# Attention from factors: the two halves of a score set on one row group, in two tiles each of F and G

## The chip, the cores and the metric

The kernel runs on one core of one Trainium2 chip. The metric is the device time of one execution in microseconds. Three runs of the kernel before took 5,615.98, 5,625.36 and 5,626.08 us; the median, 5,625.36, is the time before.

## What is computed

The reference is a network of four layers on an input of 4 images, 128 channels, 64 x 64 points, in float32. Layer 0 is a deformable convolution, layer 1 a convolution with a scan in two directions, layer 2 an attention by cosines, a feed-forward block and a mixture of experts; layer 3 has the attention that is changed here, and another mixture of experts. That attention, on 4,096 tokens an image with 128 channels, after a layer norm of the tokens, is

```python
f = jnp.einsum('bih,ha->bia', x, W1[:h])
g = jnp.einsum('bjh,ha->bja', x, W1[h:])
t = jnp.tanh(f[:, :, None, :] + g[:, None, :, :] + b1)
scores = jnp.einsum('bija,a->bij', t, w2[:, 0]) + b2[0]
flag = jnp.tril(jnp.ones((n_seq, n_seq), dtype=x.dtype), -1)[None, :, :]
e = jnp.exp(scores) * flag
denom = jnp.sum(e, axis=-1, keepdims=True) + 1e-10
w = e / denom
return jnp.einsum('bij,bjh->bih', w, x)
```

with 16 values of a. Every token looks at all earlier ones, so the tanh would be wanted at 16 x 4,096 x 4,096 / 2 places of each image.

## The kernel before

**The way of computing.** With E = exp(2(f + g + b1)), tanh is 1 - 2 / (E + 1), and E is a product of a factor of token i and a factor of token j. The 16 values of a are split into three sets, of 6, 5 and 5 (ATT_SETS, L67). For each set the sum of w2 / (E + 1) is written as one fraction: the common denominator is a sum over all subsets of the set (64, 32 and 32 terms), and each term is again a factor of i times a factor of j. So the denominators of a block of 128 x 512 scores are a matrix product of F (128 rows of terms by 512 tokens) with G, and the numerators one of F with N, where N is G with each row multiplied by the weights of that subset (cw). Rows 0 to 63 of these tiles belong to the first set, 64 to 95 to the second, 96 to 127 to the third. `attention_maps` (L1907) makes the maps from tokens to exponents, wf and wg, and cw, once.

**Products.** A product runs on 32 rows of the PE array, and four products on four different groups of rows can run at once. The second and third set take one product each. The first set has 64 rows and takes two, rows 0 to 31 and rows 32 to 63, whose results are added in one PSUM bank. [...]an order is needed. It goes through SyncE: a `nop` on SyncE, `between` (L2150), waits for the first half of both the denominators and the numerators (`leads`), and the second halves (`ends`) wait for that `nop`. The matmuls of float32 appear in the profile as two passes, so each product of the code has two rows there.

**Steps.** An image has eight row blocks ib of 512 tokens; row block ib has 4 ib + 3 steps (`blocks`, L2113), one for each 128 x 512 block of scores with the blocks on the diagonal cut and joined. That is 136 steps an image and 544 in all, and 7 more at the end. `step` (L2261) calls `products` (L2122) for a block, and carries older blocks on:

- den: the denominators of this block, four products into three of D's four banks. The second and third set always use banks 1 and 2. The first set uses bank 0 or bank 3 (`side` 0 or 1).
- num: the numerators of the block before, four products into num1 and num2 (three banks, one buffer).
- ScalarE: Ln of the three banks of D, into the tile r, and Exp of minus that, which is one over each denominator. A fourth quarter of the same tile holds the finished sum of an older block, so one Exp of 2,048 columns does both.
- VectorE multiplies r with num2, then num1. POOL adds the three quarters into another tile r. On the diagonal VectorE then multiplies the finished weights by the mask `keep`.
- `weigh` (L2212): one product of the weights with the tokens into acc, over the whole row block.
- `settle` (L2225), once for each row block: transposes into D's bank 3, a copy zs, and the division by the denominator in VectorE.

All engines work in program order in this stage, except that POOL, VectorE, ScalarE and TensorE wait for each other where tiles or banks demand it; `held_to` and its callers say by hand which Ln a product must wait for.

**Preparation.** The next row block's F, G and N are made in six parts (`prepare`, L2078), spread over the steps of the present row block: 0 statistics (every second block), 1 the normalised tokens v, 2 four transposes into bank 3 and the copy vT, 3 the product of wf with vT and F = exp, 4 the largest value of F for the later test of size, then the product of wg and G, 5 the largest value of G, then N = G * cw on POOL. A part that uses bank 3 (2, 3, 4, `ON_BANK`, L2258), as settle does, makes a step "taken":

```python
taken = held[-1] is not None or any(p in ON_BANK for p in parts)
side = int(last[0] == 0 and not taken and not last[1])
again = side == last[0]
```

A taken step and the one behind it have side 0. Where side is the same as in the step before (`again`), den writes the bank that the last Ln reads and waits for it. The order of the products depends on it: without `again` the second and third set of den come last; with it they come before the second halves.

The number of the part that has to be done by round r is `to` (L2283): 6 parts over all rounds of the row block, in the last row block over the rounds from the 11th.

Of the kernel before, what the change touches and what calls it, by code (L numbers as in the profile page):

```python
# [16 lines left out]
P = 128  # L17
# [45 lines left out]
ROW, NROWS = _places(ROWS)  # L63

# [23 lines left out]
class Kernel:  # L88
# [1818 lines left out]
    def attention_maps(self, ctx):  # L1907
# [5 lines left out]
        with tc.tile_pool(name="r3a", bufs=2, space=PSUM) as aux, tc.tile_pool(name="r3w", bufs=1) as wp:  # L1913
# [7 lines left out]
            wf = cp.tile([P, P], F32, name="wf")  # L1921
            wg = cp.tile([P, P], F32, name="wg")
            cw = cp.tile([P, 1], F32, name="cw")
# [3 lines left out]
            with tc.tile_pool(name="r3m", bufs=1) as mp:  # L1927

                pi = mp.tile([P, 6], I32, name="pi")
                bits = mp.tile([P, 6], F32, name="bits")  # L1930
                nc.gpsimd.iota(pi, pattern=[[0, 6]], base=0, channel_multiplier=1)
                for k in range(6):
                    nc.vector.tensor_scalar(pi[:, k:k + 1], pi[:, k:k + 1], k, 1,
                                            ALU.arith_shift_right, ALU.bitwise_and)
                nc.vector.tensor_copy(bits, pi)
                has = mp.tile([P, 2, 16], F32, name="has")
                nc.vector.memset(has, 0.0)
                for hs, a0, a1 in ATT_SETS:
                    nc.vector.tensor_copy(has[hs, 0, a0:a1], bits[hs, 0:a1 - a0])
                    nc.vector.tensor_scalar(has[hs, 1, a0:a1], bits[hs, 0:a1 - a0], -1.0, 1.0,  # L1940
                                            ALU.mult, ALU.add)
# [10 lines left out]
                for k in range(4):  # L1952
                    src = has[:, k, :] if k < 2 else wd[:, k - 2, :]
                    nc.tensor.transpose(ps[0:16, k * P:(k + 1) * P], src, self.ident)
                nc.vector.tensor_copy(sel.rearrange("p k c -> p (k c)"), ps[0:16, :])

# [3 lines left out]
                nc.vector.tensor_add(sel[:, 3, :], sel[:, 3, :], bl)  # L1960

                w2 = w2z[0:16, 24:25]
                ps = aux.tile([P, 512], F32, name="aux")
                nc.tensor.matmul(ps[:, 0:P], sel[:, 2, :], sel[:, 0, :], start=True, stop=True)
                nc.tensor.matmul(ps[:, P:2 * P], sel[:, 3, :], sel[:, 0, :], start=True, stop=True)
                nc.tensor.matmul(ps[:, 2 * P:2 * P + 1], sel[:, 1, :], w2, start=True, stop=True)
                nc.vector.tensor_copy(wf, ps[:, 0:P])
                nc.vector.tensor_copy(wg, ps[:, P:2 * P])
                nc.vector.tensor_scalar(cw, ps[:, 2 * P:2 * P + 1], 2.0, None, ALU.mult)
# [13 lines left out]
    def attention(self):  # L1983
# [14 lines left out]
        with ExitStack() as outer:  # L1998
# [7 lines left out]
            with ExitStack() as ctx:  # L2006
# [44 lines left out]
                top = cp.tile([P, NB * 8, 2], F32, name="top")  # L2051
# [26 lines left out]
                def prepare(n, q):  # L2078
# [18 lines left out]
                    out = {"v": v}  # L2097
                    for k, (to, m) in enumerate((("F", wf), ("G", wg))):
                        ps = aux()
                        aside(nc.tensor.matmul(ps, m, vT, start=True, stop=True))  # L2100
                        t = bp.tile([P, 512], F32, name=f"{to}_{q}")
                        uses[:] = [nc.scalar.activation(t, ps, AF.Exp, scale=2.0)]
                        wrote[0] = t
                        out[to] = t
                        yield
                        nc.vector.tensor_reduce(top[:, 8 * n + q, k:k + 1], t, AX.X, ALU.max)
                    w = bp.tile([P, 512], F32, name=f"N_{q}")
                    nc.gpsimd.tensor_scalar(w, t, cw, None, ALU.mult)
                    out["N"] = w
# [12 lines left out]
                def products(block, side, again, before, summed):  # L2122
# [6 lines left out]
                    now, new = spaces.pop(0), rp.tile([P, 4, 512], F32, name="r", bufs=7)  # L2129
                    spaces.append(new)  # L2130
                    if block is not None:
                        n, ib, parts, end = block
                        cs = slice(parts[0][2].start, 512)
                        dv = D[:, side:side + 3, :]
                        den = pieces[n, ib]["F"], [pieces[n, t // 4]["G"] for t, _, _ in parts], parts, \
                            D[:, 3 * side, :], [D[:, k, :] for k in (1, 2)]
                    if before is not None:
                        n0, ib0, parts0, end0, cs0, side0, r0 = before
                        n1 = pp.tile([P, 512], F32, name="num1")
                        n2 = pp.tile([P, 2, 512], F32, name="num2")  # L2140
                        num = pieces[n0, ib0]["F"], [pieces[n0, t // 4]["N"] for t, _, _ in parts0], parts0, \
                            n1, [n2[:, k, :] for k in (0, 1)]

                    def product(x, out, row, start=True, stop=True):
                        rows = slice(row, row + 32)
                        return [nc.tensor.matmul(out[:, c], g[rows, t % 4 * P:(t % 4 + 1) * P], x[0][rows, i],
                                                 start=start and k == 0, stop=stop, skip_group_check=True)
                                for k, (g, (t, i, c)) in enumerate(zip(x[1], x[2]))]

                    between = nc.sync.nop()  # L2150
                    leads, ends = [], []

                    def ready(x):
                        if x is not None:
                            for k in range(2):
                                for op in product(x, x[4][k], 64 + 32 * k):
                                    if x is den:
                                        other_sets(op, [x[0], *x[1]])

                    for to, second, todo in ((leads, False, ((den, 0), (num, 32))),  # L2160
                                             (ends, True, ((num, 0), (den, 32)))):
                        if second and again:
                            ready(den)
                        for x, row in todo:
                            if x is not None:
                                ops = product(x, x[3], row, start=not second, stop=second)
                                to += ops
                                for op in ops:
                                    if x is den:
                                        first_set(op, side, [x[0], *x[1]])  # L2170
                        if not second:
                            ready(num)
                        elif not again:
                            ready(den)
                    for op in leads:
                        tc.add_manual_dep(between.ins, op.ins.name, ENDED, reason="one bank, other rows")
                    for op in ends:
                        tc.add_manual_dep(op.ins, between.ins.name, ENDED, reason="one bank, other rows")
# [31 lines left out]
                acc = [None]  # L2210

# [44 lines left out]
                spaces = [rp.tile([P, 4, 512], F32, name="r", bufs=7) for k in range(2)]  # L2256
                held = [None] * len(later)
                PARTS, ON_BANK = 6, (2, 3, 4)  # L2258
# [230 lines left out]
```

## Time and profile before

| What | Value |
|---|---|
| Median of three runs | 5,625.36 us |
| The profiled execution, its own time | 5,626.52 us |
| Its span | 5,624.8 us |
| Mean granted clock of TensorE in the span | 0.944 |
| TensorE busy | 5,034.6 us (90%) |
| VectorE busy | 3,967.9 us (71%) |
| ScalarE busy | 3,095.8 us (55%) |
| POOL busy | 3,025.3 us (54%) |
| Attention of layer 3, 3,072 to 5,238 us: TensorE busy | 2,031.49 us of 2,166 |
| the same, ScalarE | 1,806.89 us |
| the same, POOL | 1,398.51 us |
| the same, VectorE | 1,286.40 us |
| the same, granted clock | 0.97 |

The profile is of one execution. Busy time is the time in which at least one instruction runs on the engine, so four products at once count once. PE are the matmuls, PEld the loads of their stationary operand. A row of the timeline gives start, length, engine, line, operation, the tile written and the tiles read, the shape, the count of instructions that were put together, and in brackets how long the engine had stood idle and which engine and tile released it. L81 is the line of the helper that records every operation of this stage, so groups are told apart by their tiles: D<-F,G are the denominators, num<-F,N the numerators, r<-D the Ln, r<-r the Exp on ScalarE and the sums on POOL, r<-r,num the products on VectorE. "SPq" is SyncE's queue.

### The profile page before, as it was taken

Reading aid. Unit: us, or ns where it says so; the run is one execution under the profiler, and the core shown is the slowest. Engines: PE = TensorE matmul, PEld = TensorE weight load, DVE = VectorE, ACT = ScalarE, POOL = GpSimd, SP = SyncE. Lnnn points to the kernel's source line nnn. Section 1 sums busy time; section 2 is a strip of 40 time slices with the busy share of each in tenths; the row PEclk is TensorE's granted clock in tenths of the full one; section 3 lists DMA queues with packets and bytes.
Section 4 is the critical chain, followed back from the end, with each engine's and each line's share of the span. In section 5 each row is a group of like instructions: output and inputs, shape, how many; then the busy total and the mean of one; then the engine's idle time right before and its main releaser. Section 6 shows DMA issues by size and latency. Waiting matters only on the chain. (4 is left out here: it accounts for less than half of the span.)

```text
span 5624.8 us, 62917 instructions
## 1 busy us (share of the span) xinstructions
PE 5034.6 (90%) x21582; PEld 2263.2 (40%) x21582; DVE 3967.9 (71%) x7776; ACT 3095.8 (55%) x3721; POOL 3025.3 (54%) x2995
## 2 busy tenths in 40 slices
PE   6898988879999859999787999899989998999787
PEld 3454444436656523333443333333333333333343
DVE  6888988758876577886697655566566565665796
ACT  1122222146655445555421788878878887889431
POOL 0525344314444334544498666666666665667597
PEclk8999999989989779999898999999999999999899
DMA  5545454300000110000000000000000000000001
GB/s 173 129 128 127 130 129 121 94 6 3 14 16 16 43 40 1 1 1 1 6 31 30 1 1 1 1 1 1 1 1 1 1 1 1 1 1 1 5 1 60
DMA packets 66746, 185.23 MB, mean 33 GB/s; under 512 B 13158, under 2 KB 16038, under 8 KB 64744
## 3 DMA queue, kind: packets, MB, share of 16 engines
q1 hardware_dynamic: 55792, 163.68, 9.9%
q0 software_dynamic: 6272, 12.86, 1.4%
q10 hardware_dynamic: 4344, 4.50, 0.3%
q8 instruction: 174, 2.85, 0.2%
q14 instruction: 164, 1.34, 0.1%
HBM read 131.63 MB, written 49.36 MB: 32 GB/s over the span
## 5 line engine op out<-in xcount | busy, mean ns | idle before, releaser
L81 POOL TENSOR_TENSOR r<-r 128x512 f32<-128x512 f32 (+1 forms) x1088 | 1349.2, 1240 | 750.8 <-DVE r L81 688.3
L81 DVE TENSOR_TENSOR r<-r,num 128x1024 f32<-128x1024 f32 (+1 forms) x1088 | 964.6, 926 | 626.7 <-PE num L81 555.6
L81 PE MATMUL num<-F,N 32*128 32x512 f32 (+3 forms) x4608 | 1227.1, 614 | 70.2 <-DVE r L81 27.9
L81 PE MATMUL D<-F,G 32*128 32x512 f32 (+3 forms) x4608 | 1247.3, 607 | 33.6 <-ACT r L81 29.9
L81 ACT ACTIVATE r<-r 128x2048 f32<-128x2048 f32 (+4 forms) x610 | 1018.4, 1679 | 50.9 <-POOL r L81 3.8
L81 ACT ACTIVATE r<-D 128x1536 f32<-128x1536 f32 (+1 forms) x544 | 767.3, 1410 | 263.8 <-PE D L81 213.6
L81 PE MATMUL acc<-pr,ident 128*128 128x512 f32 x1600 | 748.3, 618 | 76.2 <-DVE pr L81 76.2
L81 PEld LDWEIGHTS D<-F,G 32*128 32x128 f32 x4608 | 415.6, 187 | 487.8 <-issue 344.9
L81 PE MATMUL acc<-r,v 128*128 128x512 f32 (+3 forms) x1152 | 608.0, 615 | 2.4 <-DVE aT L81 2.4
L1885 PE MATMUL pex<-w_expert_w,vT 128*128 128x512 f32 x1024 | 489.6, 617 | 79.5 <-DVE x L1888 79.4
L81 PEld LDWEIGHTS num<-F,N 32*128 32x128 f32 x4608 | 357.1, 186 | 468.5 <-SPq L81 340.1
L1895 POOL TENSOR_TENSOR x<-x 128x512 f32<-128x512 f32 (+2 forms) x576 | 472.5, 820 | 105.8 <-DVE x L1888 75.8
L81 PEld LDWEIGHTS acc<-pr,ident 128*128 128x128 f32 x1600 | 309.1, 198 | 435.9 <-issue 339.8
L81 DVE TENSOR_TENSOR pr<-v,wt 128x2560 f32<-128x2560 f32 x160 | 452.5, 2833 | 30.1 <-PE acc L81 24.3
L81 PE MATMUL pff<-hid,w_ffn_w2T 128*128 128x512 f32 x1024 | 468.2, 600 | 0.0
L81 POOL DMA_INDIRECT px<-tab,idx x196 | 331.8, 1693 | 227.8 <-DVE idx L81 159.2
L1888 DVE TENSOR_TENSOR x<-pex,gate 128x1024 f32<-128x1024 f32 x256 | 308.8, 1212 | 61.8 <-POOL X L1896 49.9
L81 POOL TENSOR_TENSOR X<-X,sl 128x512 f32<-128x512 f32 x32 | 87.7, 2740 | 491.8 <-ACT sl L81 491.8
L81 PEld LDWEIGHTS acc<-r,v 128*128 128x128 f32 x1152 | 177.1, 191 | 392.5 <-POOL r L81 217.3
L81 ACT ACTIVATE hid<-phh,cols 128x512 f32<-128x512 f32 x320 | 198.9, 685 | 223.9 <-PE phh L81 223.9
L1885 PEld LDWEIGHTS pex<-w_expert_w,vT 128*128 128x128 f32 x1024 | 183.2, 193 | 330.3 <-DVE x L1888 181.6
L81 POOL TENSOR_TENSOR Y<-y,tm 128x64 f32<-128x64 f32 x256 | 115.9, 473 | 323.4 <-DVE w L81 160.7
(562 smaller groups left out, 7139.3 us busy)
## 6 DMA issues: line engine op xcount, KB each, us to landing
v<-tab SPq DMA_DIRECT2D x320, 256.0 KB
oms<-omw SPq DMA_DIRECT2D x32, 432.0 KB
omr<-oms SPq DMA_DIRECT2D x32, 432.0 KB
X<-in_x_dram SPq DMA_DIRECT2D x8, 1024.0 KB
tab<-vb SPq DMA_DIRECT2D x64, 128.0 KB
o<-o SPq DMA_DIRECT2D x32, 256.0 KB
oin<-o SPq DMA_DIRECT2D x32, 256.0 KB
kept<-X SPq DMA_DIRECT2D x4, 2048.0 KB
```

Source lines behind the costliest of these rows:

```text
L81: return lambda *args, **kwargs: self.tc.keep_in_program_order(op(*args, **kwargs))
L1885: nc.tensor.matmul(pex[:, 4 * h:4 * h + 4, :], vT[:, k, :], ew[:, 512 * h:512 * (h + 1)], start=True, stop=True)
L1888: nc.vector.tensor_tensor(x, pex, gate[:, k, :].unsqueeze(2).to_broadcast([P, NE, P]), ALU.mult)
L1895: nc.gpsimd.tensor_tensor(x[:, 0:w, :], x[:, 0:w, :], x[:, w:2 * w, :], ALU.add)
```

## The change

The first set is split by its sixth member instead of by rows. Tile F0 and G0 hold, on rows 0 to 31, the 32 subsets without that member, F1 and G1 those with it. Rows 32 to 63 hold the same once more, multiplied by cw in G: so rows 0 to 31 serve the denominators and rows 32 to 63 the numerators of the first set. Rows 64 to 127 hold the second and third set in both; G0 keeps them as they are, for the denominators, and G1 has them multiplied by cw, for the numerators. N is gone: POOL multiplies G0 and G1 in place by two columns cw, which are 1 where nothing is to be multiplied.

The two halves of the first set are then two products on the same 32 rows, added in one bank one behind the other. The `nop` on SyncE and the waits for it are gone. In a step without `again` the order of the products is den half 0, num half 0, num's other sets, den half 1, num half 1, den's other sets. With `again` it is num half 0, num's other sets, den half 0, den half 1, num half 1, den's other sets.

A piece needs four products of a map with vT, four Exp, four reductions for the test of size and two products on POOL, where it needed two, two, two and one. There are eight parts instead of six: 2 transposes and vT, 3 F0, 4 F1, 5 G0, 6 G1 and the product of G0 with cw, 7 the product of G1. Parts 2 to 6 use bank 3. F0 and F1 have three buffers in turn, G0 and G1 one for each of the eight row blocks. The steps are the same, 544 and 7.

```diff
-                    for k, (to, m) in enumerate((("F", wf), ("G", wg))):
+                    for k, (to, m) in enumerate((("F", wf[0]), ("F", wf[1]), ("G", wg[0]), ("G", wg[1]))):
                         ps = aux()
                         aside(nc.tensor.matmul(ps, m, vT, start=True, stop=True))
-                        t = bp.tile([P, 512], F32, name=f"{to}_{q}")
+                        t = bp.tile([P, 512], F32, name=f"{to}{k % 2}" + (f"_{q}" if to == "G" else ""),
+                                    bufs=1 if to == "G" else 3)
                         uses[:] = [nc.scalar.activation(t, ps, AF.Exp, scale=2.0)]
...
                         nc.vector.tensor_reduce(top[:, 8 * n + q, k:k + 1], t, AX.X, ALU.max)
-                    w = bp.tile([P, 512], F32, name=f"N_{q}")
-                    nc.gpsimd.tensor_scalar(w, t, cw, None, ALU.mult)
-                    out["N"] = w
+                        if to == "G":
+                            nc.gpsimd.tensor_scalar(t, t, cw[k % 2], None, ALU.mult)
...
-                    between = nc.sync.nop()
...
-                    for op in leads:
-                        tc.add_manual_dep(between.ins, op.ins.name, ENDED, reason="one bank, other rows")
-                    for op in ends:
-                        tc.add_manual_dep(op.ins, between.ins.name, ENDED, reason="one bank, other rows")
+                    def first(x, half):
+                        if x is not None:
+                            product(x, x[3], 0 if x is den else 32, half, start=half == 0, stop=half == 1)
+
+                    def others(x):
+                        if x is not None:
+                            for k in range(2):
+                                product(x, x[4][k], 64 + 32 * k, 0 if x is den else 1)
+
+                    if again:
+                        first(num, 0)
+                        others(num)
+                        first(den, 0)
+                    else:
+                        first(den, 0)
+                        first(num, 0)
+                        others(num)
+                    first(den, 1)
+                    first(num, 1)
+                    others(den)
...
-                PARTS, ON_BANK = 6, (2, 3, 4)
+                PARTS, ON_BANK = 8, (2, 3, 4, 5, 6)
```

In `attention_maps` the maps are made twice, for the two values of the sixth member:

```diff
+                for b in range(2):
+                    nc.vector.memset(bits[:, 5:6], float(b))
+                    for hs, a0, a1 in ATT_SETS:
+                        nc.vector.tensor_copy(has[hs, b, 0, a0:a1], bits[hs, 0:a1 - a0])
...
+                for b in range(2):
+                    ps = aux.tile([P, 512], F32, name="aux")
+                    for k, m in enumerate((wf, wg)):
+                        nc.tensor.matmul(ps[:, k * P:(k + 1) * P], maps[:, k, :], sel[:, 2 * b, :],
+                                         start=True, stop=True)
+                        nc.vector.tensor_copy(m[b], ps[:, k * P:(k + 1) * P])
+                    nc.tensor.matmul(ps[:, 2 * P:2 * P + 1], sel[:, 2 * b + 1, :], w2, start=True, stop=True)
+                    nc.vector.memset(cw[b], 1.0)
+                    for hs in ((slice(32, 64),), (slice(32, 64), slice(64, 128)))[b]:
+                        nc.vector.tensor_scalar(cw[b][hs, :], ps[hs, 2 * P:2 * P + 1], 2.0, None, ALU.mult)
```

The largest values are kept in four columns of `top` instead of two. Everything outside the attention of layer 3 and its maps is as it was, one line further down.

## The prediction

> **What bounds the kernel now.** I read the slices of the page first (TensorE granted nearly full speed from 3,150 us on, no DMA to speak of), then the attention stage by itself, since nearly all of the change is there: its first product starts at 3,079.9 us and its last sum at 5,236 us, about 2,166 us of the span. The costliest groups of ScalarE in that stretch, by shape (line, operation, count | busy us, mean ns | idle before):
>
> ```profile
> L81 ACT ACTIVATE r<-r 128x2048 f32<-128x2048 f32 x478 | 913.3, 1911 | 44.9 <-ACT r L81 1.5
> L81 ACT ACTIVATE r<-D 128x1536 f32<-128x1536 f32 x512 | 741.8, 1449 | 248.2 <-PE D L81 213.6 <-DVE vT L81 19.9 <-DVE r L81 8.3
> ...
> L81 ACT ACTIVATE F<-D 128x512 f32<-128x512 f32 x32 | 18.7, 583 | 24.0 <-PE D L81 24.0
> ```
>
> Each step has one Ln (r<-D) and one Exp (r<-r). The Ln waits for TensorE in 214 us of the stage: one engine is full in some steps, the other in others. So I took the timeline of one ordinary step, late in an image (start, length, engine, operation, count):
>
> ```profile
> 5151.12 1.45 ACT L81 ACTIVATE r<-D 128x1536 f32<-128x1536 f32 x1 [1.48 <-PE D L81]
> ...
> 5152.01 0.69 PE L81 MATMUL D<-F,G 32*128 32x512 f32 x1
> ...
> 5152.66 1.91 ACT L81 ACTIVATE r<-r 128x2048 f32<-128x2048 f32 x1
> 5153.27 0.18 PEld L81 LDWEIGHTS num<-F,N 32*128 32x128 f32 x1 [0.94 <-SPq L81]
> ...
> 5154.34 1.13 PE L81 MATMUL acc<-r,v 128*128 128x512 f32 x2
> 5154.50 1.45 ACT L81 ACTIVATE r<-D 128x1536 f32<-128x1536 f32 x1
> ...
> 5155.39 0.69 PE L81 MATMUL D<-F,G 32*128 32x512 f32 x1
> ```
>
> A step is three rounds of TensorE: four row groups at once (from 5152.01), after SyncE's signal the second four (5153.27), then acc (5154.34), and the next step at 5155.39. The intervals are 1.26, 1.07 and 1.05 us: SyncE's hop costs 1.26 - 1.07 = **0.185 us** a step, and the step is 3.38. ScalarE in the same stretch: Ln to Exp 1.542, and from Exp to the next Ln at least 1.815 wherever nothing else holds it, together **3.357 us**. The ordinary step is thus bound by TensorE with ScalarE 0.025 us behind it. That is the main fact of this case: the hop can give back 0.185, but an ordinary step only shows 0.025 of it.
>
> The other kind is a step that must write D where the Ln before still reads ("again", L2266), with an auxiliary product behind it:
>
> ```profile
> 4115.78 1.45 ACT L81 ACTIVATE r<-D 128x1536 f32<-128x1536 f32 x1
> ...
> 4117.28 0.69 PE L81 MATMUL D<-F,G 32*128 32x512 f32 x1 [0.54 <-ACT r L81]
> ...
> 4118.53 0.18 PEld L81 LDWEIGHTS num<-F,N 32*128 32x128 f32 x1
> ...
> 4119.74 1.45 ACT L81 ACTIVATE r<-D 128x1536 f32<-128x1536 f32 x1 [0.51 <-PE D L81]
> ...
> 4120.56 1.02 PE L81 MATMUL D<-vT,wf 128*128 128x512 f32 x2
> ...
> 4121.51 0.69 PE L81 MATMUL D<-F,G 32*128 32x512 f32 x1
> ...
> 4123.10 0.58 ACT L81 ACTIVATE F<-D 128x512 f32<-128x512 f32 x1
> 4123.96 1.45 ACT L81 ACTIVATE r<-D 128x1536 f32<-128x1536 f32 x1 [0.29 <-PE D L81]
> ```
>
> From Ln to Ln 3.96 us: TensorE starts when the Ln ends and needs both rounds; then, with the product of F between, 4.21. Third, after each new row block three steps with masked columns (4.59, 4.24, 5.06) and one after settle (4.92) wait for VectorE, which frees num late; TensorE's two rounds and the Ln follow. Reading all 544 Ln starts and sorting the steps by the rules of step: row blocks 3 to 7 hold 296 ordinary steps (mean 3.42), 34 again behind a product (4.22), 30 other again (4.02), 100 steps of masks and settle; blocks 0 to 2 take 409 us for 84 steps.
>
> **The change part by part.** *The hop.* Both halves of den's first set now run on rows 0 to 31, of num's on 32 to 63, so their order comes from TensorE itself. A trace has no such pair; bounds: 0.185 us a step is gained, or nothing, if the second half's weights wait for the first half. The Trainium skill ("TensorE: Matmul & The Clock Gate", part 3, "The mechanism") speaks for nothing: weight loads overlap running matmuls only when their row groups differ. A load is 0.18 us (5153.27 above), so by the rule the hop is replaced by its like (a second weight buffer, which the same section also names, would lift it). But in the again step den's other sets go on rows 64 to 127 right behind num's, their weights load at 4117.83 us while those rows are busy, and they start at 4118.26, 0.43 us behind num's last pass. I take the row: 0.185. SyncE's queue holds only these signals in the stage, so nothing behind them moves. By the rule the sum below would be 36 us worse. Where it is on the path in blocks 3 to 7: 64 again steps and 100 of masks and settle, 164 x 0.185 = **-30**. Ordinary steps: 244 x 0.025 = **-6**.
>
> *Two products more per piece.* 32 pieces now make F0, F1, G0, G1: 64 more products (0.95 us of TensorE: 4120.56 to 4121.51), 64 more Exp of 0.58, 64 more reductions of 0.68 on VectorE, 32 more POOL products of 1.57. POOL has 0.74 us free in a step of 3.38 and N's step took 3.38 to 3.40 before, so POOL's is nothing (now it also waits for the reduction of the same tile, which ends before POOL's own two sums of that step do); uncovered it would be 50 us. All 64 Exp on the path would be 37 us, all products 61.
>
> *The bank.* Parts 2 to 6 of 8 use D's fourth bank instead of 2 to 4 of 6, and a step with such a part, and the one behind it, must take side 0. Walking the loop by its own rule for `to`, again steps go from 147 to **241**: per image, by row block, 2, 5, 7, 4, 3, 6, 6, 5 before and 2, 7, 8, 10, 10, 8, 8, 9 after. Of the 94 new ones, 28 fall on steps of masks or settle and cost nothing there: the wait for VectorE ends later than the Ln (second Ln at 4049.12, num's products at 4049.82). 14 are in blocks 0 to 2, below. 52 replace ordinary ones at 3.39. 18 of these have no product ahead: Ln 1.45, two rounds of 1.07 and two signals, 3.78, +0.39 each: **+7**. 34 stand behind a product: TensorE needs acc 0.97, product 0.95, two rounds 2.14, 4.03 with no lead; ScalarE 1.542 + 1.816 + 0.598 = 3.96. An ordinary step now leaves TensorE 0.15 us ahead, so I take 4.00, between the two: 34 x 0.61 = **+21**, and **-1** on the 34 of that kind there were. Putting num ahead of den in again steps moves num's products before the Ln's end, but Ln needs den's two rounds after it: nothing.
>
> *Row blocks 0 to 2*, followed step by step. Block 0 gets three parts a step: F0, F1, G0 behind each other in one bank, each waiting for the Exp of the one before (1.0 + 0.6 us and signals), but transposes and vT leave a step earlier: +1 an image. Block 1: vT no longer stands behind the mask: -2. Block 2: G0 now meets settle in one step and waits for zs, as the transposes do in block 4 before (5.31 against 3.94): +1.4, less the hop: +1.2 net. Together **+1**. The meeting of block 4 moves to block 6, nothing.
>
> *The rest.* Reductions and vT that fall into masked steps lengthen VectorE's chain there by 0.68 in some six places: **+4** (nothing to 20, if each of 28 were on the path). The maps take some 14 more operations of 0.16 us once: **+2**.
>
> Sum: -30 - 6 + 7 + 21 - 1 + 1 + 4 + 2 = **-2**. The profiled execution took 5,626.5 us (span 5,624.8), 1.2 above the median, so 5,624.5 there and **5,623** as a median: no change. What a measurement can tell from no change is about 0.2%, 11 us.
>
> **Rivals.** *Faster: the stalls at the start of the images go.* Blocks 0 to 2 take 409 us for 84 steps, 317 if each were a clean again step of 3.78. TensorE stands for 3 us there (4160.6 to 4163.6, for vT) and is then granted half speed; such spells sum to some 75 us from 3,150 us on, most of them at these places. If vT's earlier start ends the stalls, a third of the 92 us goes: about 5,592. Against it: three products in a row bring gaps of 1 us each. *Slower: the bank decides.* If added again steps cost the 0.6 us of 3.96 to 4.03 everywhere, masked steps too, 94 x 0.6 = 56 instead of 28: 5,651. It decides from 36 / 94 = 0.38 us per added again step. For it: again behind again leaves TensorE no lead. *The order costs as much as the hop*: the weights wait, -36 becomes 0: 5,659.
>
> **How the numbers follow.** The sum's case 0.43, spread of 12 us either way (0.10 of it faster, 0.27 same, 0.06 slower); stalls go 0.33; the bank 0.16; the weights 0.08. Faster 0.43, same 0.27, slower 0.30. The range reaches to the middle of both sides: 5,588 to 5,655; the sum's own is 5,611 to 5,635.
>
> **What would show it.** Ln to Ln 3.36 in ordinary steps with no idle before the Ln; second round 1.07 behind the first; again steps 3.78, behind products 3.96 to 4.03; 241 of them; block 0 longer, block 1 shorter. Second rounds 1.25 behind the first would make the weights' case; ordinary steps at 3.38 too. A granted clock near 1.00 through the first blocks would make the faster one.

## The result, and the profile after

The median went from 5,628.13 us (10 runs, 5,611.88 to 5,641.41) to **5,599.39 us** (10 runs, 5,581.55 to 5,613.62): a ratio of 0.9947, 95% interval 0.993 to 0.9965, so 29 us faster. The profiled execution has a span of 5,599.5 us, 25.3 below the one of before. The page of the changed kernel begins so:

```profile
span 5599.5 us, 62830 instructions
...
PE 4991.9 (89%) x21718; PEld 2404.9 (43%) x21718; DVE 4016.3 (72%) x7854; ACT 3113.9 (56%) x3785; POOL 3073.1 (55%) x3027
```

TensorE is busy 43 us less although it has 136 more passes (21,718 against 21,582), 128 of them for the doubled preparation; every other engine is busier, by 18 to 48 us. The groups of ScalarE in the attention of layer 3, by shape (line, operation, count | busy us, mean ns | idle before, and what ended it):

```profile
L82 ACT ACTIVATE r<-D 128x1536 f32<-128x1536 f32 x512 | 738.8, 1443 | 199.4 <-PE D L82 174.2 <-DVE vT L82 14.0
...
L82 ACT ACTIVATE G<-D 128x512 f32<-128x512 f32 x64 | 37.2, 581 | 10.2 <-PE D L82 10.1
L82 ACT ACTIVATE F<-D 128x512 f32<-128x512 f32 x64 | 37.2, 581 | 21.7 <-PE D L82 21.7
```

The idle time before the Ln fell from 248.2 to 199.4 us, and ScalarE took on 37 us of Exp for the preparation. Now the timeline of an ordinary step:

```profile
5144.13 1.43 ACT L82 ACTIVATE r<-D 128x1536 f32<-128x1536 f32 x1
5144.39 0.69 PE L82 MATMUL D<-F,G 32*128 32x512 f32 x1
...
5144.93 0.59 PE L82 MATMUL D<-F,G 32*128 32x512 f32 x1
...
5145.35 0.59 PE L82 MATMUL D<-F,G 32*128 32x512 f32 x1
...
5146.68 1.12 PE L82 MATMUL acc<-r,v 128*128 128x512 f32 x2
...
5147.48 1.43 ACT L82 ACTIVATE r<-D 128x1536 f32<-128x1536 f32 x1
5147.73 0.69 PE L82 MATMUL D<-F,G 32*128 32x512 f32 x1
```

The two rows at 5144.39 and 5144.93 are the two passes of the first half, the one at 5145.35 begins the second half on the same rows. It stands 0.96 us behind the first half, where it stood 1.26 behind in the kernel before; and acc comes 1.33 us after that row. Both rounds together take 5146.68 - 5144.39 = 2.29 us here, since den's other sets wait until the Ln at 5144.13 has left their banks (1.43 us later). TensorE has time for that now: the Ln has no idle time before it. Where TensorE is late the rounds are shorter, as the step that writes the bank of the Ln before ("again"), behind an auxiliary product, and the ordinary step after it show:

```profile
3908.59 1.43 ACT L82 ACTIVATE r<-D 128x1536 f32<-128x1536 f32 x1
...
3908.76 1.02 PE L82 MATMUL D<-vT,wg 128*128 128x512 f32 x2
...
3910.08 0.69 PE L82 MATMUL D<-F,G 32*128 32x512 f32 x1
...
3910.61 0.59 PE L82 MATMUL D<-F,G 32*128 32x512 f32 x1
3910.61 0.18 PEld L82 LDWEIGHTS D<-F,G 32*128 32x128 f32 x1 [0.17 <-issue]
...
3912.41 1.44 ACT L82 ACTIVATE r<-D 128x1536 f32<-128x1536 f32 x1
...
3913.04 0.69 PE L82 MATMUL D<-F,G 32*128 32x512 f32 x1
...
3914.01 0.59 PE L82 MATMUL D<-F,G 32*128 32x512 f32 x1
...
3914.97 1.13 PE L82 MATMUL acc<-r,v 128*128 128x512 f32 x2
```

From Ln to Ln it is 3.82 us, 4.21 before. The ordinary step behind it has both rounds in 3914.97 - 3913.04 = **1.93 us**, against 1.26 + 1.07 = 2.33 before. The second half begins at 3914.01, so the two rounds take 0.97 and 0.96 us, where each took 1.07 before and the signal came on top: the passes on rows 0 to 31 follow each other by 0.53, then 0.43 and 0.43, where every round before began anew with 0.53. The 0.40 us are more than twice what the hop was priced at.

All 544 Ln starts, sorted as in the prediction, give this for row blocks 3 to 7 (medians, us from Ln to Ln):

| Step | before | after | predicted |
|---|---|---|---|
| ordinary | 3.38 | 3.34 | 3.36 |
| again, no product ahead | 3.96 | 3.59 | 3.78 |
| again, behind a product | 4.21 | 3.84 | 4.00 |
| first step of a row block, blocks 5 to 7 | 3.32 | 2.22 | not named |
| the step behind settle | 4.92 | 4.92 | 4.74 (4.92 less the hop) |

The fourth row was not foreseen. The step before a new row block is only half as wide (768 columns of Ln). (In the code num is two blocks behind den, not one: `waiting` has two places.) Here is the first step of row block 6 in the second image, in the kernel before, from the half Ln to the next full one:

```profile
3937.20 0.81 ACT L81 ACTIVATE r<-D 128x768 f32<-128x768 f32 x1
...
3938.08 0.69 PE L81 MATMUL D<-F,G 32*128 32x512 f32 x1
...
3939.34 0.71 PE L81 MATMUL D<-F,G 32*128 32x512 f32 x3
...
3940.56 1.45 ACT L81 ACTIVATE r<-D 128x1536 f32<-128x1536 f32 x1 [1.15 <-PE D L81]
```

and the same place after:

```profile
3936.19 0.69 PE L82 MATMUL D<-F,G 32*128 32x512 f32 x1
3936.29 0.79 ACT L82 ACTIVATE r<-D 128x768 f32<-128x768 f32 x1
...
3938.51 1.45 ACT L82 ACTIVATE r<-D 128x1536 f32<-128x1536 f32 x1
```

ScalarE needs only 2.22 us for the half step. Before, TensorE's full step of 3.38 stood in its place (1.15 us idle before the Ln); after, TensorE has started the next block 0.1 us before the half Ln, out of a lead it has gained in the steps before, and the Ln waits for nothing. All first steps of blocks 3 to 7 together went from 66.3 to 49.5 us.

### The profile page after: what moved, and what is told of

Same layout as the page of the kernel before. It is cut to its first block, busy times and chain, and to the rows that moved or that the text cites. A ratio compares the mean times of both kernels' runs of the same rounds, so it can differ in the third digit from the quotient of the medians.

```text
span 5599.5 us, 62830 instructions
## 1 busy us (share of the span) xinstructions
PE 4991.9 (89%) x21718; PEld 2404.9 (43%) x21718; DVE 4016.3 (72%) x7854; ACT 3113.9 (56%) x3785; POOL 3073.1 (55%) x3027
## 5 line engine op out<-in xcount | busy, mean ns | idle before, releaser
L82 PE MATMUL D<-F,G 32*128 32x512 f32 (+3 forms) x4608 | 1218.8, 589 | 1.9 <-POOL G L82 1.0
L82 PE MATMUL num<-F,G 32*128 32x512 f32 (+3 forms) x4608 | 1084.5, 604 | 105.4 <-DVE r L82 101.6
L82 PEld LDWEIGHTS D<-F,G 32*128 32x128 f32 x4608 | 507.2, 189 | 327.4 <-issue 217.2
L82 PEld LDWEIGHTS num<-F,G 32*128 32x128 f32 x4608 | 394.4, 187 | 410.9 <-DVE r L82 239.5
```

The lines of the kernel that those rows point to most:

```text
L82: return lambda *args, **kwargs: self.tc.keep_in_program_order(op(*args, **kwargs))
```

## Where the time went

The attention, from first Ln to last, went from 2,141.5 to 2,106.8 us, -34.7. By place: row blocks 0 to 2 -2.1; then, in row blocks 3 to 7, first steps -16.8, second and third +4.1, the fourth to ninth (masks and settle) -5.5; and from the tenth on, 70 steps that are again now and were not +22.6, 30 that were and are -11.6, 26 that were and are ordinary now -19.3, the other 154 ordinary ones -6.1. The stretch ahead of the first Ln was 13.3 us longer in this execution and the one behind the last 3.9 shorter, which makes the 25.3 of the spans. Of the 13.3, some 6 belong to the change: from the first product of a map with vT to the first Ln it is 15.6 us, 9.9 before, for the first piece needs four products and four Exp before the first step can begin, instead of two. (With these 6 the change is -29, as in the medians.) The rest has no cause that the record shows: that first product came at 3,065.9 to 3,092.0 us over all kernels here, in no order of the edits. So stages, not spans, are compared below, beside medians.

## The experiments

Two theories were open. One: the hop is worth what was measured at it, and the doubled preparation takes most of it back. The other: the gain is somewhere else, in the new order of the products or in the stalls at the start of the images.

### The hop put back, and the preparation halved

`e_hop` is the changed kernel with a SyncE signal again between the first and second halves:

```diff
+                            if row < 64 and half == 0:
+                                tc.add_manual_dep(between.ins, op.ins.name, ENDED, reason="hop")
+                            elif row < 64:
+                                tc.add_manual_dep(op.ins, between.ins.name, ENDED, reason="hop")
...
+                    between = nc.sync.nop()
```

> The changed kernel with SyncE's hop put back between the first and the second halves of the first set; nothing else differs, and the result does not need it. Theory Q (queue: what the change gains is that the second round of products stands in TensorE's queue right behind the first and its passes follow at 0.43 us instead of 0.53, so the hop cost more than its own 0.185): again steps go from 3.59 back to 3.96, those behind a product from 3.84 to 4.21, ordinary ones from 3.34 to 3.38, the first step of a row block from 2.2 to 3.3; about 116 x 0.37 + 244 x 0.04 + 20 x 1.1 = 75 us more, 5,675. Theory H (hop alone: 0.185 a step, the rest of the gain comes from the new order of the products in again steps): again 3.78 and 4.03, about 30 us more, 5,630.

Measured: 5,711.17 us (4 runs), ratio 1.0159 (1.0129 to 1.0189); the stage 2,209.5, which is 102.7 over the changed kernel (112 in the medians). Theory Q had the kind right and the size too small, by 36 us. The timeline of one step of it:

```profile
5144.15 0.69 PE L82 MATMUL D<-F,G 32*128 32x512 f32 x1
...
5145.41 0.18 PEld L82 LDWEIGHTS D<-F,G 32*128 32x128 f32 x1 [0.94 <-SPq L82]
...
5146.48 1.13 PE L82 MATMUL acc<-r,v 128*128 128x512 f32 x2
```

1.26 and 1.07 us, exactly the kernel before. With the signal the first pass of the second round takes 0.53 again until the next; without it that round follows the passes ahead of it at 0.43. Again steps are back at 3.95 and 4.27, ordinary ones at 3.38, the first steps at 67.1 us instead of 49.5.

`e_halfprep` asks the other side: the changed kernel with F1 and G1 not made. F0 and G0 stand in for them, so part of the denominators and numerators is left out, but every product of a step runs as in the changed kernel.

```diff
-                    for k, (to, m) in enumerate((("F", wf[0]), ("F", wf[1]), ("G", wg[0]), ("G", wg[1]))):
+                    for k, (to, m) in enumerate((("F", wf[0]), ("G", wg[0]))):
...
-                        out[to].append(t)
+                        out[to] += [t, t]
...
-                PARTS, ON_BANK = 8, (2, 3, 4, 5, 6)
+                PARTS, ON_BANK = 6, (2, 3, 4)
```

> F1 and G1 are left out: each piece makes one F and one G (six parts, bank 3 in parts 2 to 4 as before), and F0 and G0 stand in for F1 and G1 in all products; the number of products, Ln and Exp in the steps stays. It prices the doubled preparation. If added again steps and added products cost what the trace of the changed kernel shows for ordinary row blocks (0.25 for an again step, 0.50 with a product ahead, over 3.34): 18 x 0.25 + 34 x 0.50 = 22 us less there, some 10 more in masked steps and blocks 0 to 2: 5,568. If they are covered: 5,595 to 5,600. If the half-speed spells of the masked steps are due to the doubled parts as well: 5,555.

Measured: 5,555.69 us (4 runs), ratio 0.9883 (0.9862 to 0.9905); the stage 2,062.0. So the hop and the closer rounds are worth 79.5 us of the stage (72 of the medians) with the preparation of before: row blocks 0 to 2 -26, first steps -20, and from the tenth step of a row block on, again steps -21.5 and ordinary ones -11.6. The doubled preparation costs 44.8 (43.7 of the medians), of which row blocks 0 to 2 have 24 and the steps from the tenth on 19. The change is **-80 + 45** in the stage, not the -36 + 34 of the prediction.

The two prices depend on each other. `e_hop`, with the hop and the doubled preparation, stands 68 us above the kernel before; so beside the hop the doubled preparation costs 68 and not 45, and beside the doubled preparation the hop is worth 103 and not 80. More again steps make the signal dearer: 41 of the 103 us lie in the 100 again steps from the tenth on.

The 5,555 that one branch of the expectation named was hit for another reason than it gave. In the fourth to sixth steps of row blocks 4 to 7 TensorE stood at half clock for 20.5 us here and for 23.9 in the changed kernel, against 4.9 in the kernel before and 3.4 in `e_hop`: in these executions the spells came with the closer rounds and not with the doubled preparation.

### The order of the products

`e_denfirst` is the changed kernel with den's first half always ahead; `e_b_numfirst` the kernel before with num ahead in again steps, and its signal kept.

```diff
-                    if again:
-                        first(num, 0)
-                        others(num)
-                        first(den, 0)
-                    else:
-                        first(den, 0)
-                        first(num, 0)
-                        others(num)
+                    first(den, 0)
+                    first(num, 0)
+                    others(num)
```

> The changed kernel with one order of the products in all steps: den's half 0 first, also in again steps, where it waits for the Ln at the head of TensorE's queue with num behind it. Theory Q: the two rounds still follow each other closely, so again steps stay at 3.59 to 3.62 and the time at 5,600 within 5 us. Theory H: the new order is what shortened the again steps, they go to 3.78 (3.84 stays where a product lies ahead), 116 steps x 0.1 to 0.19, 5,612 to 5,620.

> The kernel before with only the order of the again steps changed: num's lead and its other sets before den's lead, as in the changed kernel; SyncE's hop stays. Theory Q: den's two rounds still come after the Ln with the hop between, again steps stay at 3.96 and 4.21, time as before, 5,628 within 6 us. Theory H: again steps fall to 3.78, 64 x 0.18 = 12 us less at least, 5,615.

Measured: 5,599.14 us (7 runs), ratio 0.9949 (0.9932 to 0.9965), beside 0.9947 for the changed kernel; and 5,630.51 us (12 runs), ratio 1.0004 (0.9992 to 1.0016). Again steps are at 3.59 and 3.84 in the first, 3.92 and 4.24 in the second. The order is worth nothing in either layout, and is no part of the gain.

### The parts in the masked steps

In the changed kernel the fourth to sixth step of a row block, those that the masks make long, have become dearer in row blocks 4 to 7: 221.1 us against 215.3, although the hop is gone. In block 6, three of them took 4.28, 4.24 and 5.06 to 6.77; in block 7, where no part falls there, 4.28, 4.24 and 4.04. Two kernels move the parts behind these steps. `e_late` spreads those of blocks 4 to 6 from the tenth step on (block 7 has its own behind them already), `e_pack` puts those of blocks 4 to 7 into eight steps in a row from the tenth (from the twelfth in block 7). The code and the expectations of these two count rounds from nought: their 9th and 11th are the tenth and twelfth step.

```diff
-                    first = 4 + LAG if ib == 7 else 0
+                    first = 4 + LAG if ib == 7 else 9 if ib > 3 else 0
```

```diff
                         to = -(-PARTS * max(r - first + 1, 0) // (rounds - first))
+                        if ib > 3:
+                            to = min(PARTS, max(r - max(first, 9) + 1, 0))
```

> The changed kernel with the parts of row blocks 4 to 6 spread as before but from the 9th round on, clear of masks and settle; 249 again steps. Masked steps: first to eighth round of these blocks from 32 to 34.5 us to block 7's 31.4. Against it, again steps and the four copies v stand in the open. If masked steps are lengthened by the parts in them: 5,590. If the parts were free there: 5,605.

> The changed kernel with the eight parts of row blocks 4 to 7 in eight steps behind each other, from the 9th round (in block 7 from the 11th), clear of the steps of masks and settle; 219 again steps instead of 241. If the bank's price is the number of again steps (0.25 each, 0.50 with a product ahead), 22 fewer save 6 to 10 us and the masked steps become those of block 7, another 5 to 8: 5,585. If parts behind each other wait for each other as in block 0 (bank, Exp, next product), each product costs 1 us more, 16 blocks x 4 x 0.5: 5,630.

Measured: `e_late` 5,606.41 us (16 runs), ratio 0.9965 (0.9949 to 0.998); `e_pack` 5,575.82 us (4 runs), ratio 0.9906 (0.9877 to 0.9935). The median of `e_late` alone would say that the masked steps are indifferent to the parts. The Ln starts of blocks 4 to 7 say otherwise:

| us in row blocks 4 to 7 | changed kernel | `e_late` | `e_pack` |
|---|---|---|---|
| steps 4 to 6 (masks) | 221.1 | 202.5 | 201.0 |
| steps from the tenth on | 895.6 | 915.4 | 904.3 |
| again steps in the whole stage | 241 | 249 | 219 |

Both take about 20 us out of the masked steps. `e_late` pays them back behind, where its parts stand apart and each makes two again steps; packed, a part's second again step is the next part's first. The 20 us are the price of all eight parts there. What the doubling added is less: `e_halfprep`, with six parts in their old places, stands at 217.3 in these steps, 3.8 below the changed kernel.

### The mask on POOL

The masks keep VectorE waiting for ScalarE 171.2 us in the changed kernel, and TensorE behind it. `e_mask_pool` and `e_b_mask_pool` are the changed kernel and the one before with the mask multiplied by POOL, which has just made the tile it multiplies:

```diff
-                                nc.vector.tensor_mul(ready_e[4][:, ds], ready_e[4][:, ds], keep)
+                                nc.gpsimd.tensor_tensor(ready_e[4][:, ds], ready_e[4][:, ds], keep, ALU.mult)
```

> The changed kernel with the diagonal's mask multiplied on POOL instead of VectorE; nothing else. If the steps of masks are long because VectorE stands at the mask until the Exp ends, with the products of num behind it (4.28, 4.24, 4.04 in rounds 3 to 5), they fall towards 3.4 to 3.6: 28 blocks x 2 to 2.5 us, 5,540. If the sums on POOL become what acc waits for, they stay near 4: 5,590.

> The kernel before with the mask on POOL, the same edit. If masked steps are bound by VectorE there too, they fall from 4.59, 4.24, 5.06 towards 3.5: 5,565. It tells whether the change is worth more or less without the masked steps: with theory Q, which sets it at about 80 us less 45 of preparation, the difference to the changed kernel with the same edit stays at 25 to 45 us.

Measured: 5,512.58 us (4 runs), ratio 0.9785 (0.9749 to 0.982), and 5,520.0 us (4 runs), ratio 0.9805 (0.9772 to 0.9837). The groups of the numerators and of the mask, first in the changed kernel:

```profile
L82 PE MATMUL num<-F,G 32*128 32x512 f32 x3840 | 980.8, 643 | 92.4 <-DVE r L82 88.7
...
L82 DVE TENSOR_TENSOR r<-r,keep 128x128 f32<-128x128 f32 x128 | 64.6, 524 | 171.2 <-ACT r L82 171.2
```

then in `e_mask_pool`:

```profile
L82 PE MATMUL num<-F,G 32*128 32x512 f32 x3840 | 967.9, 636 | 47.0 <-DVE r L82 44.4
...
L82 POOL TENSOR_TENSOR r<-r,keep 128x128 f32<-128x128 f32 x128 | 57.2, 458 | 67.7 <-ACT r L82 65.3 <-DVE r L82 2.1
```

POOL's wait is the smaller, and it holds up almost nobody (what waits for the mask itself there waits 4.5 us in all). VectorE, freed of it, multiplies by num earlier, and TensorE waits half as long for num's banks, 44.4 us instead of 88.7. The mask's mean of 524 ns on VectorE hides a spread, too: the median is 293, but the one at 4,052.22 us, between two masked steps, took 1.12 us; on POOL all take 447 to 494 ns. What makes some slow on VectorE was not asked. In row blocks 6 and 7 the three long steps fall from 4.28, 4.24 and 4.04 or more to 3.34, 3.16 and 3.34 us. This one line is worth 87 us to the changed kernel and 108 to the one before, three times the change itself and more than either expectation had (5,540 and 5,565). But with it the change is worth only 7 us in the medians, and the intervals overlap (the stages of the two profiled executions differ by 19). The expectation had it stay at 25 to 45, which makes a new question: why does the same change bring 29 us beside one mask and next to nothing beside the other?

### Is the cover gone?

In row blocks 0 to 2 the change brought -2.1 us with the mask on VectorE and **+27.9** with the mask on POOL; everywhere else it brought -33 and -47. One theory: in those short row blocks the doubled preparation lay beside the waits for the masks, and is bare once they are gone. `e_half_mask_pool` is `e_halfprep` with the mask on POOL (the same part of the computation is left out).

> The changed kernel with the diagonal mask on POOL, and with the preparation at its old size: F1 and G1 are not made, F0 and G0 stand in for them in both halves of the first set, so part of the denominators is left out. The pair with the masks on POOL (before 5,520, changed 5,512.6) showed a gain of only 7 us where the pair with the masks on VectorE showed 29. Theory A, the cover is gone: the doubled preparation of row blocks 0 to 2 lay beside the waits for VectorE's mask and is now bare, while the hop is worth what it was, some 80 us: about 5,440, so that the doubled preparation costs some 72 us here against 45 with the masks on VectorE. Theory B, the hop is worth less once the masked steps are short, and preparation costs its 45: about 5,468.

Measured: 5,416.96 us (4 runs), ratio 0.9634 (0.9609 to 0.9658); the stage 1,934.5. That is the first theory, and beyond it: the hop is worth 103 us of the medians (101.1 of the stage, 24.4 of them in row blocks 0 to 2), and the doubled preparation costs 96 (82.2 of the stage, 52.3 of them in row blocks 0 to 2, where it cost 23.9 with the mask on VectorE). The timeline of `e_mask_pool` shows it bare, in the third step of the second image, between the Ln at 3,615.36 and the half Ln at 3,624.30 us, with F0, F1 and G0 to make:

```profile
3618.72 0.58 ACT L82 ACTIVATE F<-D 128x512 f32<-128x512 f32 x1
...
3619.35 1.13 PE L82 MATMUL D<-vT,wf 128*128 128x512 f32 x2 [2.13 <-ACT F L82]
3620.52 0.60 ACT L82 ACTIVATE F<-D 128x512 f32<-128x512 f32 x1 [1.22 <-PE D L82]
...
3621.17 1.12 PE L82 MATMUL D<-vT,wg 128*128 128x512 f32 x2 [0.69 <-ACT F L82]
3622.24 0.69 PE L82 MATMUL D<-F,G 32*128 32x256 f32 x2
3622.33 0.60 ACT L82 ACTIVATE G<-D 128x512 f32<-128x512 f32 x1 [1.22 <-PE D L82]
...
3624.30 0.81 ACT L82 ACTIVATE r<-D 128x768 f32<-128x768 f32 x1 [1.37 <-PE num L82]
```

Product, Exp, product, Exp, product through one bank: TensorE and ScalarE wait for each other in turn, and the step's own products come at 3622.24. Ln to Ln it takes 8.9 us; the kernel before with the same mask needs 5.8 there. In row block 1 the statistics and v of a piece now fall into one step, and TensorE waits for v:

```profile
3634.37 0.30 ACT L82 ACTIVATE rstd<-rstd,eps 128x8 f32<-128x8 f32 x1 [2.91 <-DVE rstd L82]
...
3635.35 1.24 PE L82 MATMUL D<-ident,v 128*128 128x128 f32 x4 [2.61 <-DVE v L82]
...
3637.06 1.22 PE L82 MATMUL D<-F,G 32*128 32x512 f32 x1
...
3638.91 1.07 PE L82 MATMUL D<-F,G 32*128 32x512 f32 x3
```

After the 2.61 us of standing still the row of three products takes 1.07 us, where the like takes 0.70 in the kernel before with the same mask: TensorE is granted half its clock from 3,635.8 to 3,642.7 us. These two steps together are 12.75 us from Ln to Ln; in the kernel before with the same mask 8.36.

So not all of the 52 us is the preparation's own work. In row blocks 0 to 2 TensorE stood at half clock for 53.8 us in `e_mask_pool`, for 28.6 in the kernel before with the same mask and for 22.9 in `e_half_mask_pool`; with the mask on VectorE the halved and the doubled preparation had it alike, 77.7 and 77.6. Passes on the same rows follow by 0.85 us at half clock and by 0.43 at full, so as an estimate at most half of the 31 us that `e_mask_pool` has above `e_half_mask_pool`, some 15, is lost to the clock. That is up to half of the 28 us by which the doubled preparation became dearer in these row blocks. No run here tells the two apart.

### What beats both

`e_best` is the changed kernel with the mask on POOL and packed parts, `e_b_pack_mask` the kernel before with the same two edits (six parts).

> The changed kernel with the diagonal mask on POOL and with the eight parts of row blocks 4 to 7 packed into eight steps one behind the other, from the tenth step of the row block. If the two savings add, 5,512.6 less the 24 us of packing: about 5,489. If part of what packing saved was that it kept parts out of the masked steps, which are short now, about 5,500.

> The kernel before with the same two edits: the mask on POOL, and its six parts of row blocks 4 to 7 packed from the tenth step. Again steps only go from 147 to 141 by the loop's own rule, so if packing saves through their number, about 5,515, and the changed kernel keeps the rest as its own gain. If packing saves by keeping parts together whatever the number, about 5,500.

Measured: 5,507.47 us (4 runs), ratio 0.9794 (0.9761 to 0.9827), and 5,508.65 us (4 runs), ratio 0.9801 (0.9771 to 0.9831). The savings do not add: with the masked steps short, taking the parts out of them saves 9.3 us instead of 20 and the steps behind pay 8.5. And the change is worth 1 us beside these two edits, which the runs cannot tell from nothing (12.6 in the stages of the two profiled executions, less the 6 ahead of them). The changed kernel came out above both times that were expected, the kernel before between its two. The last kernel, `e_early`, moves the bare preparation. In images 1 to 3 a piece is made one row block sooner: row block 7 of the image before makes two pieces, and row blocks 0 and 1 share one.

```diff
+                ahead = (x for piece in order[1:] for x in prepare(*piece))
...
+                        if ib == 7:
+                            to = base + min(2 * PARTS, max(r - 3 - LAG, 0)) if n + 1 < NB else done
+                        elif ib > 3:
+                            to = base + min(PARTS, max(r - 8, 0))
+                        elif n and ib == 0:
+                            to = base + PARTS + r + 1
+                        elif n and ib == 1:
+                            to = base + 3 - (-(PARTS - 3) * (r + 1) // rounds)
+                        else:
+                            to = base - (-PARTS * (r + 1) // rounds)
...
```

> The changed kernel with the mask on POOL and packed parts, as in the run at 5,507, and in images 1 to 3 the preparation moved one row block ahead: row block 7 of the image before makes two pieces (16 parts in a row from its twelfth step), row blocks 0 and 1 share one. If the bare preparation of row blocks 0 to 2 is what eats the change's gain, row blocks 0 and 1 of images 1 to 3 come down from some 53 us an image to some 40, and eight more parts in row block 7 cost 2 to 3 us an image: about -31, 5,476. If those row blocks are held by something else (the pipeline's own start at an image, the transposes of settle), they stay and the run is at 5,507 or above it.

Measured: **5,470.17 us** (5 runs), ratio 0.9719 (0.9701 to 0.9737), 37 us below `e_best`, 129 below the changed kernel. Row blocks 0 and 1 of images 1 to 3 came down from 159.7 to 111.4 us, and row block 7 of the images ahead of them went up from 324.6 to 333.9. Here, too, the clock has a share: TensorE stood at half clock for 40.1 us in row blocks 0 to 2, for 70.4 in `e_best`. The step of row block 1 that took 6.6 us takes 3.9 here, with one product beside its own:

```profile
3611.97 1.45 ACT L82 ACTIVATE r<-D 128x1536 f32<-128x1536 f32 x1 [0.77 <-PE D L82]
...
3612.79 1.02 PE L82 MATMUL D<-vT,wf 128*128 128x512 f32 x2
...
3615.86 1.45 ACT L82 ACTIVATE r<-D 128x1536 f32<-128x1536 f32 x1
```

Whether the kernel before would gain as much from the same move was not tried; its preparation is the smaller, and its row blocks 0 and 1 stood at 130.9 us in images 1 to 3 with the mask on POOL.

## Why the prediction was right, and where its steps were not

The forecast was 5,623 in a range of 5,588 to 5,655; the time is 5,599, in the range, but faster by 0.5% where the sum said no change. The sum was -36 + 34; the runs show -80 + 45 in the stage and +6 ahead of it. Both sides were too small, and 44 us of error on the one met 17 on the other. The sum's own spread, 5,611 to 5,635, missed; the wide range held since it reached halfway to the rivals, so luck has a part in it.

**The hop, -30 - 6.** The mechanism was right: no signal, no wait for weights (the rival that rested on one rule of the Trainium skill falls: the second half's pass follows at 0.43 us on the very rows that are in use). The step that failed in it is the term "**0.185**". It took off the signal and left both rounds at 1.07 us, where they measure 0.97 and 0.96. The 0.43 stood in the prediction's own row (den's other sets, 0.43 behind num's last pass), used to show that weights do not wait, and not used to price the rounds. 0.185 for the signal and about 0.1 for each of the two rounds make the 0.4 that was measured. The places were too few as well: first steps of row blocks (-20 us in `e_halfprep`) and row blocks 0 to 2 (-26) were given nothing or little, while 100 steps of masks and settle were given 18 of the 30 us and gave 3.5 (fourth to ninth steps, `e_halfprep`). In row block 7 the three masked steps went from 4.59, 4.24 and 4.04 to 4.28, 4.24 and 4.04: only one of the three became shorter, for the chain through VectorE's mask holds the others.

**Again steps, +7 + 21 - 1.** Their durations were 0.16 to 0.19 us too long in the forecast, mostly for the same reason (and the forecast's 4.03 for TensorE is 4.06 when its terms are added), and so was their price over an ordinary step: 3.59 - 3.34 = 0.25 and 3.84 - 3.34 = 0.50, not 0.39 and 0.61. At these prices the 18 and 34 net added ones make 22 us, not 28.

**Row blocks 0 to 2, +1.** Measured -2.1, but this is a gain of 26 and a cost of 24 (`e_halfprep`). Block 1 shrank as foreseen (156.6 to 148.1 us, -8.5 where -2 an image makes -8). Block 0 grew by more than foreseen (63.8 to 73.5, 9.7 for 4), and block 2 shrank (187.7 to 184.4) where 5 more were expected.

**Parts in masked steps, +4.** This held: 3.8 us in row blocks 4 to 7 (221.1 against 217.3 in `e_halfprep`), from one execution of each. That all parts together cost 20 there, old and new, was no part of the sum.

**The first piece, put at nothing.** Its two more products and two more Exp lie bare ahead of the first step, 5.7 us; the sum had only +2 for the maps.

**POOL, nothing.** Held in the ordinary step: 3.34 us is ScalarE's time, with no idle time before its Ln, while POOL has 100.0 us of products with cw instead of 50.1.

**The rivals.** "Stalls go" named a time close to the measured one, 5,592, but not the cause: the three short row blocks gave 2 of its 31 us, and time at half clock from 3,150 us to the end of the attention rose from 75 to 92 us. "The bank decides" needed the hop's whole 36 us to be eaten by 94 again steps; the hop was worth 80. "The order costs as much as the hop" is refuted by the 0.43 us.

What stays open: the split of the stage's -35 among single steps is from one execution of each kernel, and the masked steps with parts differ among images (5.06 or 6.77 in the same step), by spells at half clock whose start is not explained step by step. How much of the preparation's price with the mask on POOL is such spells is open as well.

## What to carry to other kernels

A signal through another queue between two rounds of matmuls costs more than its own latency: here it also kept the rounds 0.1 us longer each, since every round's first pass took 0.53 us and not 0.43; price the whole of both rounds from a row where such products already follow each other without a wait. Work that costs nothing beside a wait is bare when that wait is removed, so the worth of two edits is measured together: here the change was worth 29 us beside one mask and 7, within the noise, beside the better one. And where a stage has short and long row blocks, work that is due "by the next block" may be cheaper in the long ones ahead: here that brought 37 us.

## What the hardware showed

Products on different groups of rows need not start in program order. In the again step of the changed kernel den's second half is ahead of num's second half in the program:

```profile
3910.61 0.59 PE L82 MATMUL D<-F,G 32*128 32x512 f32 x1
...
3910.67 0.59 PE L82 MATMUL num<-F,G 32*128 32x512 f32 x1
...
3910.68 0.95 PE L82 MATMUL D<-F,G 32*128 32x512 f32 x3
...
3911.10 0.59 PE L82 MATMUL num<-F,G 32*128 32x512 f32 x1
```

Rows 0 to 31 are busy with den's first half until its second pass, at 3910.61; num's second half on rows 32 to 63 starts at 3910.67, 0.37 us ahead of den's, at 3911.04 (the last of the three that the row of 3910.68 puts together; the other two are den's other sets). The Trainium skill ("TensorE: Matmul & The Clock Gate", part 3, "The mechanism") has matmuls start and end in the program's order; here the starts keep it within a group of rows only, and the measurement decides. (The ends of matmuls are modelled in the profile, so they say nothing.)

And weights for rows in use are loaded ahead of time. Passes of 512 columns on the same rows follow by 0.43 us, and a pass of 384 columns is followed by the next after 0.32 (3,115.85 to 3,116.17 us): the same time for a column, with no room for a load of 0.18 us between them. One rule of the same section lets a load overlap only on other rows; what it says of a background weight buffer agrees with these passes.
